# Linear attention with a two-of-eight expert network: rows of the second batch taken in pairs of one expert, with 256 moving columns

## The chip, the cores and the metric

The kernel runs on one core of a Trainium2 chip. The metric is the device time of one execution in microseconds (us), the median of several runs. The core has five engines that run at the same time, each on its own list of instructions: TensorE (PE, with the loads of its stationary operand shown apart as PEld), VectorE (DVE), ScalarE (ACT), GpSimd (POOL) and SyncE (SP), which issues DMA transfers. PE writes its results to PSUM; the kernel divides it into eight banks of 128 partitions by 512 float32 values, from which DVE and ACT read.

## What is computed

The input x has 8 sequences of 1024 tokens with 256 values each, so 8192 tokens, all in float32. The output is x plus an attention plus an expert network, both applied to the layer norm of x:

```python
xn = _layernorm(x, axis=-1)
# attention, 16 heads of 16 values
q = jax.nn.elu(xn @ Wq.T) + 1.0
k = jax.nn.elu(xn @ Wk.T) + 1.0
kv_cumsum = cumsum(k outer v, along the sequence)
out = q . kv_cumsum / clip(q . cumsum(k), 1e-06)
attn = out @ Wo.T
# experts: the two best of eight by logits, weights by a softmax over the two
y_e = (_silu(xn @ W1[e]) * (xn @ W3[e])) @ W2[e]      # 256 -> 512 -> 256
ffn = sum over the two experts of weight * y_e
return x + attn + ffn
```

The reference computes every expert for every token and weights most with zero. The kernel computes only the two chosen ones, so each token gives two rows of work, 16384 rows in all, which have to be sorted by expert.

## The kernel before

**Blocks and tiles.** Attention goes over 16 blocks of 512 tokens (NBLK, TB). The expert network goes over row tiles: 128 rows of one expert. Since each expert's last tile may be part empty, there are NF = 135 of them; the last NR = 3 are in a branch at the end that is taken only if they are needed, so that NM = 132 run. They come in two batches. The first has N1 = 25 tiles and holds rows of the first four blocks only, so that the expert network can start while the routing of the other blocks is still being computed. The second has N2 = 110 and is planned by `second_batch` (L696), a list of small DVE operations on counts of rows per expert (`left`, `upto`, `past`, `room`) and of matmuls (held_ps, L725) that give for each place of each tile its token.

**A row tile, step j of the main loop** (`ffn_step`, L1237). Step j issues: the gathers of tile j+3 (`ffn_load`, two indirect DMAs on POOL: the rows xg, L1145, and their norm and weight, entry, L1150); the two weight matrices of tile j+2 (`ffn_weights`, 512 KB each on SP's queue, five buffers w13); gate and up of tile j (`ffn_hidden`); the turning of tile j+1 (`ffn_turn`, two transposes xg_t on PE, L1166, and a copy xgT on ACT, L1168); the second matrix of tile j-1 (`ffn_out`, y_ps, L1218, then the scaling y on DVE, L1225); and the store of a finished tile (`ffn_store`, an indirect DMA on POOL that adds, L1229). Gate and up are 16 matmuls of 128 moving columns into two PSUM banks (gu_ps, L1199). In float32 each matmul is two PE instructions, so that is 32. ACT reads the gate's bank with Silu (L1207) and DVE multiplies it with the up bank into hT (L1210), which is what frees that bank.

**Attention** is a generator of 11 steps a block (`block_steps`, L993), 176 in all. `attend_upto` (L1021) advances it to a given step; the main loop calls it once a row tile, ahead of `ffn_step`. A block's first steps project q, k and v (zq L795, zkk and zkv L811, then Relu, Exp and products on ACT and DVE, L762 to L765) and its denominators: den (L880) is stored to DRAM as den_d and read back as rden through SP's queue. Then follow four chunks of 128 tokens. `scores` (L909) puts 16 PE instructions of scores into four banks at once (s_ps, L919); DVE masks each bank (s_sb, L926), which frees it; it also updates the state (kv_ps L934 on PE, kv L939 and L941 on DVE). `weigh` (L945) forms o_ps (L953, L960), and DVE multiplies it with rden into oT (L967). `attend` (L972) multiplies oT with the output matrix (a_ps, L979); ACT copies it (L984) and POOL adds a block to the output.

**PSUM.** ps_mm has four banks, shared in turn by gu_ps, s_ps, zq, zkk and zkv. ps_y has two, for y_ps and a_ps (and held_ps). ps_t has two, for xg_t, tp, kv_ps and o_ps. A matmul into a bank waits until the reader of the bank's content before has finished.

**The order.** Each engine works through its instructions in one fixed order. It comes from the order in the program and from a scheduler that may move instructions in the first part; what is marked by `in_order`, the DMAs on SP among it, stays as written. Normalising the blocks 4 to 15 (`turn`, L324, and its store of xnT to DRAM, L346) and their routing go on in the first 12 row steps; `second_batch` follows in ten steps from step 12 (LISTS, READ). From READ on, the steps of attention are spread evenly over the row tiles:

```python
attend_upto(AHEAD + (NBLK * STEPS - AHEAD) * (j - READ + 1) // (NM - READ - 4))
if j == N1 + 1:
    copied.append(j)
    in_order(nc.sync.dma_start(out=out_rows[0 : FT * P, :], in_=acc_d[:, :]))
ffn_step(j, LATE if N1 < j <= N1 + LATE else 0)
```

## Time and profile before

| | |
|---|---|
| device time, median of 3 runs | 1349.92 us (1348.86 to 1350.81) |
| the profiled execution: its own time, its span | 1333.92 us, 1332.0 us |
| granted TensorE clock | 0.992 |
| PE, PEld busy | 1279.3 us (96%), 1094.5 us (82%) |
| DVE, ACT, POOL busy | 635.0, 516.5, 528.2 us |
| DMA | 240.36 MB, mean 180 GB/s |
| loads of w1 and w3 | 264 of 512 KB |
| longest wait of PE, at the start | 11.0 us, tp L333 for DVE xb L313 |

All durations below come from one profiled execution, which has its own time; the span runs from its first to its last instruction. The busy time of an engine is a sum over instructions, and a share of it says nothing yet on what sets the end. Groups of instructions are written as line, engine, operation, output and inputs by the program's names, shapes, count, then busy time and mean duration. Matmuls overlap in the engine's pipeline, so the mean duration of one is longer than the distance from one to the next. In a list of waits, "A <- B: total, times, longest" says how long A's engine stood idle until B had finished. A chain of waits gives start, duration and what ran, followed back from an end; a timeline lists each group with, in brackets, the idle time before it and what ended it.

### The profile page before, as it was taken

To read this page: it belongs to the slowest core of one execution; us is meant where nothing else is said; L and a number is where in the kernel's file an instruction comes from. 1 tells how busy PE (TensorE), PEld (TensorE's weight loads), DVE (VectorE), ACT (ScalarE), POOL (GpSimd) and SP (SyncE) were. 2 spreads that over 40 slices of the span, in tenths; PEclk is the share of its full clock that TensorE was granted. 3 is DMA by queue.
4 is the path that set the end of the run, shared out by engine and by line. 5 is a ranking of instruction groups with operands and counts; after the bars stand their busy time and mean duration, and the time that the engine had idled before them with its cause. 6 is when DMAs were issued, how large, how long until landed. Compare 5 with 4: busy or idle time off the path is not lost.

```text
span 1332.0 us, 28306 instructions
## 1 busy us (share of the span) xinstructions
PE 1279.3 (96%) x10968; PEld 1094.5 (82%) x10968; DVE 635.0 (48%) x1436; ACT 516.5 (39%) x1052; POOL 528.2 (40%) x460
## 2 busy tenths in 40 slices
PE   5799999999999999999999999999999999999996
PEld 4578787878888788888888888888888888888885
DVE  7867498753353425353443535253533534252531
ACT  4666373531515142342516152432425151524321
POOL 3634433333334334344344434344344343343432
PEclk9999999999999999999999999999999999999998
DMA  9898756566776667576666766675766676576663
GB/s 339 276 297 238 201 162 180 127 179 174 205 201 169 173 142 204 134 195 166 151 188 144 201 164 178 160 195 146 176 165 150 176 175 183 144 198 148 179 163 76
DMA packets 163462, 240.36 MB, mean 180 GB/s; under 512 B 16098, under 2 KB 87394, under 8 KB 163042
## 3 DMA queue, kind: packets, MB, share of 16 engines
q1 hardware_dynamic: 119938, 184.31, 44.4%
q0 software_dynamic: 38064, 43.22, 20.1%
q10 hardware_dynamic: 5328, 11.01, 2.3%
q8 instruction: 90, 1.47, 0.4%
q14 instruction: 42, 0.34, 0.1%
HBM read 196.30 MB, written 52.67 MB: 187 GB/s over the span
## 4 chain that ended last, share of the span: by engine, by line
PE 86%; DVE 8%; DMA 3%; SPq 1%; issue 1%; ACT 1%; POOL 0%; POOLq 0%; DVEq 0%; ACTq 0%
PE gu_ps L1199 35%; PE y_ps L1218 16%; PE s_ps L919 6%; PE o_ps L960 4%; PE a_ps L979 4%; PE zq L795 4%; PE zkk L811 4%; PE zkv L811 3%; PE xg_t L1166 2%; PE kv_ps L934 2%; DVE s_sb L926 2%; PE o_ps L953 2%; DMA xb<-in_x_dram 2%; DVE ksum L863 1%; DMA acc_d<-in_x_dram 1%
## 5 line engine op out<-in xcount | busy, mean ns | idle before, releaser
L1199 PE MATMUL gu_ps<-xgT,w 128*128 128x128 f32 x4224 | 512.4, 278 | 4.6 <-DVE s_sb L926 2.8
L1199 PEld LDWEIGHTS gu_ps<-xgT,w 128*128 128x128 f32 x4224 | 492.3, 192 | 29.4 <-issue 15.7
L1145 POOL DMA_INDIRECT xg<-in_x_dram,src_i x132 | 131.9, 999 | 451.9 <-ACT xgT L1168 361.2
L1218 PE MATMUL y_ps<-w_sb,hT 128*128 x1056 | 251.8, 381 | 2.8 <-DVE hT L1210 2.5
L1229 POOL DMA_INDIRECT out_dram<-y,dst_i x107 | 173.8, 1624 | 164.8 <-DVE y L1225 71.5
L1210 DVE TENSOR_TENSOR hT<-gu_ps,hT 128x512 f32<-128x512 f32 x132 | 91.1, 690 | 272.0 <-PE gu_ps L1199 254.5
L1218 PEld LDWEIGHTS y_ps<-w_sb,hT 128*128 128x128 f32 x1056 | 190.7, 191 | 25.5 <-DVE hT L1210 2.7
L1207 ACT ACTIVATE hT<-gu_ps 128x512 f32<-128x512 f32 x132 | 78.8, 597 | 334.9 <-PE gu_ps L1199 332.7
L926 DVE TENSOR_TENSOR s_sb<-s_ps,causal 128x512 f32<-128x512 f32 x256 | 162.7, 682 | 52.6 <-PE s_ps L919 49.8
L1225 DVE TENSOR_SCALAR y<-y_ps,entry 128x256 f32<-128x256 f32 x132 | 63.6, 482 | 145.3 <-PE y_ps L1218 145.2
L1150 POOL DMA_INDIRECT entry<-tab_d,of_i x107 | 110.0, 1028 | 36.8 <-issue 31.7
L1168 ACT COPY xgT<-xg_t 128x256 f32<-128x256 f32 x132 | 49.1, 372 | 157.8 <-PE xg_t L1166 152.6
L919 PE MATMUL s_ps<-qm,kT 32*128 32x256 f32 x1024 | 95.4, 406 | 1.4 <-DVE hT L1210 0.4
L984 ACT COPY at<-a_ps 128x256 f32<-128x256 f32 x64 | 23.8, 371 | 170.7 <-PE a_ps L979 170.7
L919 PEld LDWEIGHTS s_ps<-qm,kT 32*128 32x128 f32 x1024 | 55.9, 183 | 31.2 <-issue 18.5
L1157 ACT ACTIVATE xg<-xg,entry 128x256 f32<-128x256 f32 x132 | 79.7, 603 | 3.6 <-DVE v L286 3.2
L1229 POOL DMA_INDIRECT acc_d<-y,src_i x25 | 43.5, 1742 | 76.9 <-DVE y L1225 47.4
L979 PE MATMUL a_ps<-wo_sb,oT 128*128 128x256 f32 x256 | 67.6, 386 | 5.6 <-DVE oT L967 5.4
L960 PE MATMUL o_ps<-s_sb,va 128*32 128x128 f32 x2048 | 72.3, 278 | 0.0
L960 PEld LDWEIGHTS o_ps<-s_sb,va 128*32 128x32 f32 x2048 | 53.2, 110 | 9.2 <-issue 0.9
L795 PE MATMUL zq<-xnT,wq_sb 128*128 128x512 f32 x128 | 60.2, 603 | 0.0
L979 PEld LDWEIGHTS a_ps<-wo_sb,oT 128*128 128x128 f32 x256 | 46.2, 190 | 16.8 <-DVE oT L967 9.7
(211 smaller groups left out, 1363.5 us busy)
## 6 DMA issues: line engine op xcount, KB each, us to landing
w<-in_w_dram SPq DMA_DIRECT2D x264, 512.0 KB
den_d<-over SPq DMA_DIRECT2D x64, 128.0 KB
rden<-den_d SPq DMA_DIRECT2D x16, 512.0 KB
xnT_d<-xnT ACTq DMA_DIRECT2D x15, 512.0 KB
xnT<-xnT_d SPq DMA_DIRECT2D x15, 512.0 KB
out_dram<-in_x_dram SPq DMA_DIRECT2D x12, 512.0 KB
out_dram<-at POOLq DMA_DIRECT2D x12, 512.0 KB, 8.2
xb<-in_x_dram SPq DMA_DIRECT2D x10, 512.0 KB
```

What stands on the lines that cost most here:

```text
L795: nc.tensor.matmul(z, lhsT=wq_sb[:, k, bass.ts(o, P)], rhs=xnTs[t][:, k, :], start=(k == 0), stop=(k == KC - 1),)
L811: nc.tensor.matmul(z[:, i, :], lhsT=xnTs[t][:, k, bass.ts(c + i, P)], rhs=wkv_sb[:, k, a, :], start=(k == 0), stop=(k == KC - 1),)
L919: nc.tensor.matmul(s_ps[r][:, hh].rearrange("p a l -> p (a l)"), lhsT=kT[rows, hh, span], rhs=qm[rows, hh, :, span], start=True, stop=True,)
L926: nc.vector.tensor_tensor(sm, s_ps[r].rearrange("p k a l -> p (k a) l"), causal_b, ALU.mult)
L960: nc.tensor.matmul(o_ps[32 * r : 32 * r + 32, hh, :], lhsT=va[:, c, 4 * hh + r, a, :], rhs=s_sb[r][:, 2 * hh + a, :], start=(first and a = ...
L979: nc.tensor.matmul(a_ps, lhsT=oT[:, hh, :], rhs=wo_sb[:, hh, :], start=(hh == 0), stop=(hh == 1),)
L1145: nc.gpsimd.indirect_dma_start(out=xg[j], out_offset=None, in_=x_rows[:, :], in_offset=bass.IndirectOffsetOnAxis(ap=src_i[:, i : i + 1], a ...
L1150: nc.gpsimd.indirect_dma_start(out=entry[j], out_offset=None, in_=table[:, :], in_offset=bass.IndirectOffsetOnAxis(ap=num_i[:, i : i + 1], ...
L1199: done = nc.tensor.matmul(ps[:, i, :], lhsT=w13[:, k, bass.ts(i, P)], rhs=xgT[j][:, k, :], start=(k == 0), stop=(k == KC - 1),)
L1210: nc.vector.tensor_tensor(hT, gu[1], hT, ALU.mult)
L1218: done = nc.tensor.matmul(y_ps, lhsT=hT[:, i, :], rhs=w2_sb[:, bass.ds(e * (IC * H) + i * H, H)], start=(i == 0), stop=(i == IC - 1),)
L1229: nc.gpsimd.indirect_dma_start(out=rows[:, :], out_offset=bass.IndirectOffsetOnAxis(ap=dst_i[:, i : i + 1], axis=0), in_=ys.pop(j), in_off ...
```

## The change

The second batch is cut in another way. ND = 48 pairs come first: two tiles of 128 rows of the same expert each. Then come 14 single tiles, the last three in the branch at the end, so 11 of them run. Where the loop went over 132 tiles, it goes over 84 units (`units`, NU): 25 singles of the first batch, 48 pairs, 11 singles.

- **A pair** has xgT and hT twice as wide, and its two weight matrices are loaded once. Gate and up have 256 moving columns. A bank then holds two of the four 128-row parts of the hidden layer, so `ffn_hidden` goes in two halves, each with one gate and one up bank, one Silu and one mult. `ffn_turn` makes four transposes and one copy; `ffn_out` makes two y_ps of eight instructions, as before.
- **Attention's steps**: the loop's single call becomes up to four for a pair, through `between`: ahead of the unit, between the halves, after the second half (ahead of `ffn_turn`), and between the two y_ps.
- **The planner** has more small operations: it counts pairs per expert, cuts them at ND, and forms starts and ends for pairs and singles apart.
- **Buffers**: entry has 12 instead of 8; the second-batch xnT has one instead of two. w13 and y keep five, xg four. Gathers run up to four tiles ahead, counted in tiles; LATE, by which stores are held back after the first batch, goes from 3 to 1.

```diff
+    ND = (2 * NT - N1 - E + 1) // 2
+    N2D = 2 * ND
...
-            xnT = (two if t == 0 else f_two).tile([P, KC, TB], F32, tag="xnT", name="xnT")
+            xnT = (two if t == 0 else f_one).tile([P, KC, TB], F32, tag="xnT", name="xnT")
...
         left = f_one.tile([P, E], F32, name="left")
         nc.vector.tensor_tensor(left, rows, taken, ALU.subtract)
-        upto = add_up(left, "upto2")
-        past = past_experts(upto, N2, f_x, "xb")
+        pairs_i = f_two.tile([P, E], I32, tag="rows_i", name="pairs_i")
+        nc.vector.tensor_copy(pairs_i, left)
+        nc.vector.tensor_scalar(pairs_i, pairs_i, 1, None, ALU.arith_shift_right)
+        pairs = f_one.tile([P, E], F32, name="pairs")
+        nc.vector.tensor_copy(pairs, pairs_i)
+        upto = add_up(pairs, "upto2")
+        nc.vector.tensor_scalar(upto, upto, float(ND), 2.0, ALU.min, ALU.mult)
+        ends = f_one.tile([P, E], F32, name="ends")
+        nc.vector.tensor_tensor(ends[:, 1:E], upto[:, 1:E], upto[:, 0 : E - 1], ALU.subtract)
+        nc.vector.tensor_copy(ends[:, 0:1], upto[:, 0:1])
+        nc.vector.tensor_tensor(ends, ends, taken, ALU.add)
+        nc.vector.tensor_tensor(left, rows, ends, ALU.subtract)
+        upto_s = add_up(left, "upto3")
+        nc.vector.tensor_scalar(upto_s, upto_s, float(N2D), None, ALU.add)
+        past = f_x.tile([P, N2, E - 1], F32, tag="xb", name="past")
+        nc.vector.tensor_copy(rows_left, upto_s[0:1, E - 1 : E])
+        parts = slice(0, N2D), slice(N2D, N2)
+        for part, ends_at in zip(parts, (upto, upto_s)):
+            n = part.stop - part.start
+            nc.vector.tensor_tensor(
+                past[:, part], cols[:, part].unsqueeze(2).to_broadcast([P, n, E - 1]),
+                ends_at[:, 0 : E - 1].unsqueeze(1).to_broadcast([P, n, E - 1]), ALU.is_ge,
+            )
         te, te_i = numbers_of(past, N2, "2")
-        nc.vector.tensor_copy(rows_left, upto[0:1, E - 1 : E])
...
+        for part, firsts_at, lasts in zip(parts, (taken, ends), (ends, rows)):
+            n = part.stop - part.start
+            room = f_two.tile([P, E - 1], F32, tag="room", name="room")
+            nc.vector.tensor_scalar(
+                room, lasts[:, 0 : E - 1], -1.0, float(ROWS), ALU.mult, ALU.add
+            )
+            nc.vector.tensor_tensor(room, room, firsts_at[:, 1:E], ALU.add)
+            nc.vector.tensor_tensor(
+                past[:, part], past[:, part], room.unsqueeze(1).to_broadcast([P, n, E - 1]),
+                ALU.mult,
+            )
+        of_tiles = f_one.tile([P, N2], F32, name="rows2")
+        nc.vector.tensor_reduce(of_tiles, past, op=ALU.add, axis=AX.X)
+        for part, first in zip(parts, (taken, ends)):
+            nc.vector.scalar_tensor_tensor(
+                of_tiles[:, part], of_tiles[:, part], first[:, 0:1],
+                cols[:, 0 : part.stop - part.start], ALU.add, ALU.add,
+            )
...
+    ffn4 = ctx.enter_context(tc.tile_pool(name="ffn4", bufs=4))
     ffn5 = ctx.enter_context(tc.tile_pool(name="ffn5", bufs=5))
-    ffn4 = ctx.enter_context(tc.tile_pool(name="ffn4", bufs=4))
-    ffn8 = ctx.enter_context(tc.tile_pool(name="ffn8", bufs=8))
+    ffn12 = ctx.enter_context(tc.tile_pool(name="ffn12", bufs=12))
...
+    units = [(j,) for j in range(N1)]
+    units += [(j, j + 1) for j in range(N1, N1 + N2D, 2)]
+    units += [(j,) for j in range(N1 + N2D, NF)]
+    NU = len(units) - NR
...
+    def ffn_turn(u):
+        n = P * len(units[u])
+        tp = ps_t.tile([P, KC, n], F32, tag="t", name="xg_t")
+        for r, j in enumerate(units[u]):
+            for k in range(KC):
+                nc.tensor.transpose(tp[:, k, bass.ts(r, P)], xg.get(j)[:, bass.ts(k, P)], ident)
+        xgT[u] = ffn2.tile([P, KC, 2 * P], F32, tag="xgT", name="xgT")[:, :, 0:n]
+        nc.scalar.copy(xgT[u], tp)
...
+    def ffn_hidden(u, between, last=False):
+        n = P * len(units[u])
+        m = TB // n
+        hT = ffn2.tile([P, IC, 2 * P], F32, tag="hT", name="hT")[:, :, 0:n]
+        for a in range(0, IC, m):
+            if a > 0:
+                between()
+            gu = []
+            for s in range(2):
+                if last and s == 1:
+                    ffn_out(u - 1, None, True)
+                ps = ps_mm.tile([P, m, n], F32, tag="mm", name="gu_ps")
+                for i in range(m):
+                    for k in range(KC):
+                        done = nc.tensor.matmul(
+                            ps[:, i, :], lhsT=ws[u, s][:, k, bass.ts(a + i, P)],
+                            rhs=xgT[u][:, k, :], start=(k == 0), stop=(k == KC - 1),
+                        )
+                        if last:
+                            in_order(done)
+                gu.append(ps)
+            half = hT[:, a : a + m, :]
+            silu = nc.scalar.activation(half, gu[0], AF.Silu)
+            if u == 0:
+                in_order(silu)
+            nc.vector.tensor_tensor(half, gu[1], half, ALU.mult)
+        del ws[u, 0], ws[u, 1]
+        hs[u] = hT
...
+    def ffn_out(u, between=None, last=False):
+        hT = hs.pop(u)
+        e = expert_of(units[u][0], mybir.EngineType.PE)
+        for r, j in enumerate(units[u]):
+            if r > 0:
+                between()
+            y_ps = ps_y.tile([P, H], F32, tag="y", name="y_ps")
...
+    def ffn_step(u, behind, between):
+        while loaded[0] < min(u + 4, NU) and units[loaded[0]][-1] - units[min(u, NU - 1)][-1] <= 4:
+            for j in units[loaded[0]]:
+                ffn_load(j)
+            loaded[0] += 1
+        if u + 2 < NU:
+            ffn_weights(u + 2)
+        if u < NU:
+            ffn_hidden(u, between, u == NU - 1)
+        if u < NU and len(units[u]) > 1:
+            between()
+        if u + 1 < NU:
+            ffn_turn(u + 1)
+        if u > 0 and u != NU - 1:
+            ffn_out(u - 1, between)
         for _ in range(2):
-            if stored[0] < j - behind:
+            if stored[0] < u - behind:
                 ffn_store(stored[0])
                 stored[0] += 1
...
-    LATE = 3
+    LATE = 1
...
         if j < LISTS:
-            attend_upto(3 + j // 2)
+            upto = [3 + j // 2]
         elif j < READ:
-            attend_upto(AHEAD - 2 * (READ - j - 1))
+            upto = [AHEAD - 2 * (READ - j - 1)]
         else:
-            attend_upto(AHEAD + (NBLK * STEPS - AHEAD) * (j - READ + 1) // (NM - READ - 4))
+            unit = units[min(j, NU - 1)]
+            n = 4 * len(unit) - 4 or 1
+            upto = [
+                AHEAD + (NBLK * STEPS - AHEAD) * (n * (unit[0] - READ + 1) + len(unit) * i)
+                // (n * (NM - READ - 4))
+                for i in range(n)
+            ]
+        goals = iter(upto)
+        attend_upto(next(goals))
         if j == N1 + 1:
             copied.append(j)
             in_order(nc.sync.dma_start(out=out_rows[0 : FT * P, :], in_=acc_d[:, :]))
-        ffn_step(j, LATE if N1 < j <= N1 + LATE else 0)
+        ffn_step(j, LATE if N1 < j <= N1 + LATE else 0, lambda: attend_upto(next(goals, 0)))
```

## The prediction

> **What bounds the kernel now.** I read first the page's busy times and costliest groups, then PE's waits, then the chain of work in one steady window, then three places where PE does lose time.
>
> From the page:
> ```profile
> PE 1279.3 (96%) x10968; PEld 1094.5 (82%) x10968; DVE 635.0 (48%) x1436; ACT 516.5 (39%) x1052; POOL 528.2 (40%) x460
> ...
> L1199 PE MATMUL gu_ps<-xgT,w 128*128 128x128 f32 x4224 | 512.4, 278 | 4.6 <-DVE s_sb L926 2.8
> L1199 PEld LDWEIGHTS gu_ps<-xgT,w 128*128 128x128 f32 x4224 | 492.3, 192 | 29.4 <-issue 15.7
> ...
> L1218 PE MATMUL y_ps<-w_sb,hT 128*128 x1056 | 251.8, 381 | 2.8 <-DVE hT L1210 2.5
> ...
> L919 PE MATMUL s_ps<-qm,kT 32*128 32x256 f32 x1024 | 95.4, 406 | 1.4 <-DVE hT L1210 0.4
> ```
> PE is busy 96% of the span; gate/up is its largest group and nearly all of its loads are covered (492.3/4224 = 117 ns each). PE's waits, by what ended them:
> ```profile
> PE a_ps L979 <- DVE oT L967: 5.4, 9, 0.9
> ...
> PE gu_ps L1199 <- DVE s_sb L926: 2.8, 3, 2.0
> PE y_ps L1218 <- DVE hT L1210: 2.5, 4, 0.9
> ```
> No wait for weights (w) is there, and past the first 50 us all waits are short. The chain of waits, 700 to 720 us (start, duration, what):
> ```profile
> 702.45 1.73 PE y_ps L1218 x8
> 704.18 0.86 PE a_ps L979 x4
> 705.04 3.43 PE zq L795 x8
> 708.47 3.57 PE gu_ps L1199 x32
> ```
> This is PE alone. From it the prices start to start: 128 moving columns 3.57/32 = 111.6 ns; 256 columns 1.73/8 = 216.1 ns; 512 columns 429 ns.
>
> PE loses time where the four score banks (s_ps) must first be read by DVE. The timeline at 320 us, a score set right behind gate/up:
> ```profile
> 320.46 0.71 PE L919 MATMUL s_ps<-qm,kT 32*128 32x256 f32 x6
> 320.64 0.69 DVE L1210 TENSOR_TENSOR hT<-gu_ps,hT 128x512 f32<-128x512 f32 x1 [5.31 <-PE gu_ps L1199]
> 321.38 1.13 PE L919 MATMUL s_ps<-qm,kT 32*128 32x256 f32 x10 [0.21 <-DVE hT L1210]
> 322.44 0.92 PE L1218 MATMUL y_ps<-w_sb,hT 128*128 x3
> ```
> The set takes 322.44 - 320.46 = 1.98 us, where a free set takes 1.11: 0.87 us lost until the mult on DVE has read the up bank. The chain at 365 us, two sets with only kv_ps between:
> ```profile
> 366.05 1.11 PE s_ps L919 x16
> 367.16 0.68 DVE s_sb L926
> 367.85 0.04 issue
> 367.89 2.92 PE s_ps L919 x16
> 370.81 0.64 PE kv_ps L934 x4
> ```
> The second set takes 2.92 instead of 1.11 (and kv_ps a little longer): 2.16 us lost. At 462 us it is the next step that is late:
> ```profile
> 462.97 0.60 DVE s_sb L926
> 463.57 0.34 DVE oT L967
> 463.91 0.04 issue
> 463.95 1.13 PE a_ps L979 x4
> ```
> a_ps waits because DVE does its masks before oT, about 0.78 us.
>
> **What the Trainium skill says.** "TensorE: Matmul & The Clock Gate", section Back-to-back issue gap: a warm matmul costs N/2.4 ns and 2.5 ns fixed. The trace has two column-times per instruction: 256/2.4 + 4.9 = 111.6 and 512/2.4 + 2.8 = 216.1. So wider matmuls save only a small fixed part; this agrees. Same page, section LDWEIGHTS: columns/1.2, 106.7 ns for 128; the trace's 117 lies just under 111.6 of streaming plus overlap, so at 128 columns loading and streaming are nearly equal, at 256 the load is half. "Trainium Kernel Development and Optimization", section Best Practices: consistent bubbles can mean that PSUM ran out; the 0.87 and 2.16 us places are that. "ScalarE: Activation LUTs", section What ACT_TABLE_LOAD costs: about 1283 ns; the trace has 1283 ns for 28 Silu loads.
>
> **The change part by part.** Counts of places come from the built instruction orders of both programs, past the first 290 us; the durations are from the profile.
>
> Gate/up of 96 row tiles become 48 pairs: removed 96 x 3.571 = 342.8 us, added 48 x 32 x 0.2161 = 331.9 us: **-10.9**.
>
> Weights: 96 of 264 loads of 512 KB go (50 MB of 240). PE waits for no load now: 0. PEld busy falls by 1536 x 117 ns = 180 us, hidden already: 0.
>
> Attention steps at half tiles move the score sets. (a) Four back-to-back pairs of sets disappear: 4 x 2.16 = **-8.6**. (b) The four places where a set comes between o_ps and a_ps go: 4 x 0.78 = **-3.1**; four waits of a_ps behind gate/up, 0.75, 0.38, 0.75 and 0.30, go too: **-2.2**. (c) gate/up followed by xg_t falls from 106 to 26 places; each carries a lag of 45 ns now: **-3.6**. (d) gate/up waiting for a mask behind kv_ps, 9 to 7 places of 0.36: **-0.7**. Together with the columns: -29.1.
>
> Against that: (e) sets directly behind a gate/up half rise from 0 to 20, at 0.87: **+17.4** (and 4 with a_ps between, 0.05 each: +0.2). A half still fills a gate and an up bank of 128x512, with Silu 0.60 and mult 0.69 us, so the price should carry over. Behind the waiting s_ps stands all of PE. Bounds: 0 if the two banks that it needs first were others, 1.5 if Silu is late as well (0.60 more). (f) xg_t behind o_ps now needs the ps_t bank of kv_ps, 10 places: DVE frees it some 2.4 us after the scores end, PE is there after 2.2 (8 places) or 1.56 (2): 8 x 0.2 + 2 x 0.86 = **+3.3**. (g) Two sets with xg_t and one y between: **+1.6**; y behind y in two banks: **+1.0**.
>
> The planner of the second batch has about 15 more small DVE operations of 0.15 to 0.16 us. DVE has no idle between 157 and 178 us, so they can show: 0 to 2.4, taken **+1.5**.
>
> Costed at nothing: Table loads on ACT, 58 to 66: 8 x 1.28 = 10.3 us on an engine that waits 332.7 us for PE ahead of Silu; uncovered, one makes a Silu 1.3 us late. The single buffer of xnT in the later normalisation: its store ends at most 6.1 us after issue and the next copy comes at least 6.1 us after; tightest spare 1.3 us, so 0 to +1. rden is queued on SP behind weights whose buffers come free only when a pair's second half is done: it takes 5.3 to 7.1 us, and in four blocks the slack shrinks to 2.6 to 4.7 us; oT is then up to 1.8 us late on DVE, with y's scaling and the next mult queued behind it. PE reads oT four us later, so 0; without that cover 4 x 1.8 = +7. POOL issues the same gathers, two at a time, and waits 361 us for ACT's copy today: 0. Fewer stores are held back (LATE 3 to 1): POOL only: 0.
>
> Sum: -29.1 + 25.0 = **-4.1 us**. The profiled execution took 1333.92 us with a span of 1332.0; the median 1349.92 lies 16.0 above it. I keep that difference: span 1327.9, profiled execution 1329.8, median **1345.8**.
>
> **Rivals.** Slower: the sets behind the halves cost more than they do today. With everything else as above, the sum turns at (29.1 - 7.6)/20 = 1.08 us per set. Place: the Silu of the half's gate on ACT, which may stand behind Exp, norms and a table load of 1.28 us; then Silu and mult are waited for in turn, 0.87 + 0.60 = 1.47, which adds 12.0: **1358**. For it: halves come at shorter distances and ACT gets 8 table loads more. Against: ACT is 39% busy and at 320 us it was the mult, not Silu, that ended last. The lost cover of rden would add up to 7 to this.
>
> Larger gain: the score banks come free earlier than I take it (half the price at the 20 places), and (f), (g) stay hidden as most short waits of this trace are: -8.7 - 5 more: **1332**. For it: the waits view puts all waits of s_ps at 0.8 us in the whole span. Against: the one place with the same order cost 0.87.
>
> No difference: the wide columns save 10.9 as worked out, but the moved steps cost as much as they free, with the waits merely changing place; **1350**, 1347.5 to 1352.5. For it: gains and losses of the moved steps (18.2 and 25.0) are nearly equal, and a 5% error in each cancels my net.
>
> **How the numbers follow.** Forecast as summed (1341 to 1350) 0.40; no difference 0.15; larger gain 0.12; slower 0.33. About 0.2%, 2.7 us, is what a measurement of this kernel can tell from no change. Faster: 0.12 + 0.33 of the forecast = 0.45; same: 0.07 + 0.13 = 0.20; slower 0.35. The range 1335 to 1361 takes in both ends of (e) but not all of rden's loss; the forecast's own is 1341 to 1350.
>
> **What would show it.** Gate/up of pairs at 216 ns start to start; sets behind a half of about 2.0 us, released by DVE's mult (right) or later ones by ACT's Silu (slower rival); no 2.9 us sets; xg_t waiting for DVE's kv; PEld busy near 915 us, 190 MB moved. I am wrong if PE starts to wait for w, for rden through oT, or for the gathers, or if the sets cost other than 0.6 to 1.1 us.

## The result: 1363.21 us, 1% slower

The changed kernel takes 1363.21 us (median of 6 runs, 1359.03 to 1371.58), the kernel before, run beside it, 1351.07 us: a ratio of 1.0099, with a 95% interval of 1.0074 to 1.0123. The prediction was 1345.8 us, faster; the time lies above its range of 1335 to 1361 us, and on the other side of the kernel before. The profiled execution of the changed kernel took 1363.07 us with a span of 1361.3.

One thing has to be known to read what follows: the kernel before takes about 1339 us in some groups of runs (a lower group) and about 1351 us in others (a higher group), and all kernels of a group shift with it, so each comparison below is with the runs of before in the same group. The profile that the prediction was made from was of the lower kind (1333.92 us), and so is the second group of experiments; the result and the other groups are of the higher. For reading the change against before I use the trace of the first experiment, called the stand-in below: the kernel before with one buffer less, which makes no difference, span 1349.7 us.

The page of the kernel after, its busy times and costliest groups:
```profile
PE 1284.0 (94%) x9432; PEld 1044.8 (77%) x9432; DVE 638.4 (47%) x1451; ACT 519.2 (38%) x1012; POOL 527.2 (39%) x460
...
PEclk9899999998999999999999999999999999999998
...
L1244 PE MATMUL gu_ps<-xgT,w 128*128 128x256 f32 (+1 forms) x2688 | 498.4, 340 | 5.8 <-DVE s_sb L957 5.0
L1244 PEld LDWEIGHTS gu_ps<-xgT,w 128*128 128x128 f32 x2688 | 429.5, 193 | 60.2 <-issue 14.0
```
Gate and up have 2688 instructions instead of 4224 and 14 us less of busy time than in the profile of before; 189.78 MB are moved instead of 240.36. But PE is busy 94% of a longer span. PE's waits, by what ended them:
```profile
PE a_ps L1010 <- DVE oT L998: 7.4, 10, 1.7
PE s_ps L950 <- issue: 6.3, 3, 5.8
...
PE s_ps L950 <- DVE hT L1255: 4.5, 19, 0.6
```
The third row is 19 of the 20 score sets behind gate/up halves, as forecast. The second holds one stall of 5.8 us and the first waits for oT of up to 1.7 us; the prediction had neither. The forecast price of a set can be read at 705 us (timeline: start, duration, instructions, then the idle time and its end):
```profile
705.42 0.71 PE L950 MATMUL s_ps<-qm,kT 32*128 32x256 f32 x6
705.59 0.69 DVE L1255 TENSOR_TENSOR hT<-gu_ps,hT 128x512 f32<-128x512 f32 x1 [3.62 <-PE gu_ps L1244]
706.34 1.13 PE L950 MATMUL s_ps<-qm,kT 32*128 32x256 f32 x10 [0.22 <-DVE hT L1255]
707.40 0.71 PE L965 MATMUL kv_ps<-va,kn 128*128 128x128 f32 x4
```
The set lasts 707.40 - 705.42 = 1.98 us, and DVE's mult releases it, exactly as at the one place of before.

**Where the time went.** I mark in each trace when row tiles 20 and 120, counted from 0, reach their y_ps. The stand-in: 302.8 and 1256.0 us. After: 317.8 and 1267.5. So 15.0 us are lost before tile 20, in a part of the program that does not yet work on a single pair, and the 100 tiles behind it, with the pairs, gain 3.5. The prediction had +1.5 for the first part (the planner) and -5.6 for the rest. It is the first part that it got wrong.

Three stretches of the first part carry the loss. Columns: stretch, its length, busy time and instructions of PE, PEld, DVE, ACT, POOL, then granted clock, DMA share and GB/s. First the kernel after, then the stand-in:
```profile
60.00:80.00 20.00, 12.32 (x86) 10.70 (x87) 9.98 (x61) 5.67 (x12) 8.26 (x8) 0.74 0.52 152
100.00:120.00 20.00, 17.82 (x132) 15.88 (x133) 14.04 (x58) 9.43 (x20) 6.13 (x6) 0.83 0.77 218
290.00:320.00 30.00, 23.60 (x160) 17.95 (x159) 15.09 (x34) 4.66 (x14) 11.35 (x11) 0.77 0.48 136
...
60.00:80.00 20.00, 16.08 (x136) 14.05 (x140) 10.36 (x56) 11.37 (x25) 4.42 (x5) 0.91 0.70 229
100.00:120.00 20.00, 20.00 (x207) 16.92 (x207) 14.07 (x54) 13.03 (x29) 7.11 (x6) 1.00 0.88 276
290.00:320.00 30.00, 27.78 (x239) 22.96 (x238) 10.56 (x19) 3.98 (x9) 7.95 (x7) 0.89 0.80 247
```
In each of them PE issues fewer instructions than the stand-in, at a lower clock. POOL is busier than there in the first and the last: 8.26 us against 4.42, and 11.35 against 7.95. This is the stretch at 300 us, in the timeline of the kernel after:
```profile
299.36 1.00 POOL L1181 DMA_INDIRECT entry<-tab_d,of_i  x1 [0.30 <-issue]
300.67 0.95 POOL L1181 DMA_INDIRECT entry<-tab_d,of_i  x1 [0.30 <-issue]
301.92 0.95 POOL L1181 DMA_INDIRECT entry<-tab_d,of_i  x1 [0.30 <-issue]
...
302.13 0.70 PE L950 MATMUL s_ps<-qm,kT 32*128 32x256 f32 x4
303.17 1.61 POOL L1280 DMA_INDIRECT acc_d<-y,src_i  x1 [0.30 <-issue]
305.09 0.98 POOL L1181 DMA_INDIRECT entry<-tab_d,of_i  x1 [0.30 <-issue]
306.38 0.95 POOL L1181 DMA_INDIRECT entry<-tab_d,of_i  x1 [0.30 <-issue]
308.01 0.60 ACT L1252 ACTIVATE hT<-gu_ps 128x512 f32<-128x512 f32 x1 [11.23 <-remote]
308.66 3.82 PE L950 MATMUL s_ps<-qm,kT 32*128 32x256 f32 x13 [5.83 <-issue]
```
The gate's matmuls end at 300.4 us by the trace, but Silu begins at 308.01, after ACT has done nothing for 11.23 us and 0.7 us after POOL's unbroken run of DMA issues has ended. PE stands for 5.83 us because Silu and the mult behind it still hold its banks. The entry gathers in this run reach tile 31, while gate and up are at tile 20: with 12 buffers of entry instead of 8 there is room for them at once, and the scheduler of the first part puts them ahead of the store.

At 62 to 68 us it is the same with another reader. PE's matmuls of the logits (lg_ps) wait for ACT's copies xnT of transposes that PE finished at 59.42 and 62.28 us; ACT makes them at 66.90 and 69.74, around the end of another unbroken run of POOL's (67.34 us):
```profile
66.90 0.59 ACT L341 COPY xnT<-tp 128x512 f32<-128x512 f32 x1 [4.83 <-remote]
...
67.54 0.65 PE L359 MATMUL lg_ps<-xnT,wr_sb 128*32 128x128 f32 x8 [4.60 <-issue]
```

### The profile page after: what moved, and what is told of

The parts are those of the page before. It is cut to its first block, busy times and chain, and to the rows that moved or that the text cites. A ratio compares the mean times of both kernels' runs of the same rounds, so it can differ in the third digit from the quotient of the medians.

```text
span 1361.3 us, 24495 instructions
## 1 busy us (share of the span) xinstructions
PE 1284.0 (94%) x9432; PEld 1044.8 (77%) x9432; DVE 638.4 (47%) x1451; ACT 519.2 (38%) x1012; POOL 527.2 (39%) x460
## 2 busy tenths in 40 slices
DMA packets 137333, 189.78 MB, mean 139 GB/s; under 512 B 14562, under 2 KB 85858, under 8 KB 136930
## 4 chain that ended last, share of the span: by engine, by line
PE 81%; DVE 9%; ACT 5%; issue 2%; DMA 1%; another core or an unknown queue 1%; POOL 0%; POOLq 0%; DVEq 0%; ACTq 0%
PE gu_ps L1244 32%; PE y_ps L1267 15%; PE s_ps L950 5%; PE o_ps L991 5%; PE a_ps L1010 4%; PE zq L826 4%; PE zkv L842 3%; PE zkk L842 3%; PE xg_t L1206 2%; PE kv_ps L965 2%; PE o_ps L984 2%; DVE hT L1255 1%; DVE s_sb L957 1%; ACT L794 1%; DVE ksum L894 1%
## 5 line engine op out<-in xcount | busy, mean ns | idle before, releaser
L1244 PE MATMUL gu_ps<-xgT,w 128*128 128x256 f32 (+1 forms) x2688 | 498.4, 340 | 5.8 <-DVE s_sb L957 5.0
L1244 PEld LDWEIGHTS gu_ps<-xgT,w 128*128 128x128 f32 x2688 | 429.5, 193 | 60.2 <-issue 14.0
L950 PE MATMUL s_ps<-qm,kT 32*128 32x256 f32 x1024 | 102.3, 417 | 10.9 <-issue 6.3
L1208 ACT COPY xgT<-xg_t 128x512 f32<-128x512 f32 (+1 forms) x84 | 41.5, 494 | 165.2 <-PE xg_t L1206 156.9
L950 PEld LDWEIGHTS s_ps<-qm,kT 32*128 32x128 f32 x1024 | 58.9, 187 | 46.2 <-issue 27.3
L1195 ACT ACTIVATE xg<-xg,entry 128x256 f32<-128x256 f32 x132 | 74.2, 598 | 4.0 <-DVE sq L303 3.0
L991 PEld LDWEIGHTS o_ps<-s_sb,va 128*32 128x32 f32 x2048 | 54.1, 110 | 11.3 <-issue 2.9
```

The costliest lines, as they stand in the source:

```text
L950: nc.tensor.matmul(s_ps[r][:, hh].rearrange("p a l -> p (a l)"), lhsT=kT[rows, hh, span], rhs=qm[rows, hh, :, span], start=True, stop=True,)
L991: nc.tensor.matmul(o_ps[32 * r : 32 * r + 32, hh, :], lhsT=va[:, c, 4 * hh + r, a, :], rhs=s_sb[r][:, 2 * hh + a, :], start=(first and a = ...
L1244: done = nc.tensor.matmul(ps[:, i, :], lhsT=ws[u, s][:, k, bass.ts(a + i, P)], rhs=xgT[u][:, k, :], start=(k == 0), stop=(k == KC - 1),)
```

## The experiments

What could have cost the time: the score sets behind the halves at more than their price; a buffer made single (xnT) or held longer (w13); rden late behind the weights; and for the first part the planner's operations, the place in memory of the weights, and POOL's list with its deeper buffers of entry. Each was timed beside the kernel before; "ratio" is to before in its group. The first group holds one buffer of xnT, the steps behind the turn, the two sizes together and rden on POOL; the second the weights, the eight buffers, the planner and all three together; the third the repetitions and the eight buffers again; the fourth the rest. The second group is the lower one. The expectations speak of theories as they stood when they were written; where they speak of chips, read groups, since the second and the third ran on the same chip and were of different kinds.

**One buffer of xnT, alone** (the kernel before with this one line):
```diff
-            xnT = (two if t == 0 else f_two).tile([P, KC, TB], F32, tag="xnT", name="xnT")
+            xnT = (two if t == 0 else f_one).tile([P, KC, TB], F32, tag="xnT", name="xnT")
```


> The kernel before with the buffer of xnT of blocks 4 to 15 alone changed from two to one. Theory (the single buffer makes ACT wait for the store, PE idles around 60 us and its clock falls): the tenth y_ps group is reached 10 to 16 us later than in the kernel before, the median is 8 to 16 us longer. Rival (the stalls at 58 to 70 us of the changed kernel have another cause, the store is hidden): within 3 us of the kernel before.

Measured: 1350.18 us, ratio 0.9999 (0.9988 to 1.0011). The rival holds: the single buffer costs nothing, as the prediction had it.

**Attention's steps behind the turn.** The changed kernel, with the call between the halves removed, so that no score set stands directly behind a half:
```diff
             if a > 0:
-                between()
...
-        if u < NU and len(units[u]) > 1:
-            between()
         if u + 1 < NU:
             ffn_turn(u + 1)
+        if u < NU and len(units[u]) > 1:
+            between()
...
-            n = 4 * len(unit) - 4 or 1
+            n = 3 * len(unit) - 3 or 1
```


> The changed kernel with three places for attention steps in a pair, none of them right behind a gate/up half: ahead of the unit, behind the transposes, between the two y_ps. Theory (20 score sets behind a half cost 0.9 us each): 10 to 18 us faster than the changed kernel, hardly any s_ps set of 2.0 us left. Rival (the sets lose their time wherever they stand, since DVE is what they wait for): within 4 us of the changed kernel, with the waits at other places.

Measured: 1341.07 us, ratio 0.9933 (0.9908 to 0.9958). Repeated beside the changed kernel itself:

> The changed kernel once more, beside the kernel before on the chip that this call gets; the kernel before takes 1351 us on one chip here and 1339 us on another. Theory (the change costs the first 300 us and the waits for oT only where PE's semaphore updates come late, which shows as fewer recorded updates of PE's semaphore than PE raises, 1266 of 1355 in the first trace): if the updates are complete in this trace, 3 to 8 us faster than the kernel before, as e5 and e6 were; if some 90 are missing, 10 to 15 us slower. Rival (the placement of the weights and the entry gathers made e5 and e6 faster): 10 to 15 us slower than before on either chip.

> The changed kernel with the attention steps behind the transposes and between the two y_ps (as in the second experiment), on the chip of this call. Theory (the 20 score sets behind gate/up halves cost 0.9 us each on any chip): 10 to 22 us faster than the changed kernel of this call. Rival (that gain belonged to the chip of the first call): under 8 us.

Measured: the changed kernel 1362.58, ratio 1.0082 (1.0055 to 1.0108), 11.3 us slower, as was expected for a trace without some 90 updates (it has 1267 of 1355; what these are comes below); the steps behind the turn 1342.93, ratio 0.9926 (0.9898 to 0.9954). Removing the 20 sets and what goes with them (one place for steps less, another moved) is worth 19.7 us, within what was expected, against 17.4 that the prediction charged for the sets. The gain comes where it should; in the first of the two runs tile 20 is at 316.3 us (317.8 in the changed kernel), tile 120 at 1245.9 (1267.5). There the wait for the mult shrinks to what is left elsewhere (waits of PE):
```profile
PE s_ps L950 <- DVE hT L1253: 3.1, 3, 1.9
```
So the price was about right, and it was a price that need not be paid. But tile 20 is as late as ever: the first part's loss has another cause.

**Two buffers of xnT and four of weights, in the changed kernel:**
```diff
-            xnT = (two if t == 0 else f_one).tile([P, KC, TB], F32, tag="xnT", name="xnT")
+            xnT = (two if t == 0 else f_two).tile([P, KC, TB], F32, tag="xnT", name="xnT")
...
-            ws[u, s] = ffn5.tile([P, KC, I], F32, tag="w13", name="w13")
+            ws[u, s] = ffn4.tile([P, KC, I], F32, tag="w13", name="w13")
```


> The changed kernel with two buffers of xnT, paid for with four instead of five buffers of weights (w13). Theory (the single xnT buffer is what costs the first 160 us): the eightieth y_ps instruction is back near 158 us from 173.6, the median 8 to 16 us below the changed kernel. Rival (the weights wait with four buffers, or the stalls are not of xnT): no gain, or PE waits for w. In both, the steady part from 340 us on stays as it is.

Measured: 1359.21 us, ratio 1.0059 (1.0035 to 1.0083), whose interval overlaps that of the changed kernel; the 8 to 16 us that were expected are not there. The two changes together do not undo the loss. Four buffers of weights were not tried alone.

**rden read through POOL's queue** instead of SP's, where it stands behind weights:
```diff
-            nc.sync.dma_start(
+            nc.gpsimd.dma_start(
```


> The changed kernel with the read of rden issued on POOL's queue instead of SP's, past no weights. Theory (oT waits for an rden that is queued behind weights): the 6.4 us that y_ps loses ahead of a_ps, and waits of a_ps for oT of up to 1.7 us, go: 5 to 7 us faster. Rival (oT is late because DVE has the masks and mults of the half tiles ahead of it): these waits stay, within 2 us.

Measured: 1404.74 us, ratio 1.0404 (1.0386 to 1.0421), some 41 us slower than the changed kernel where 5 to 7 us of gain were expected, with this among PE's waits:
```profile
PE a_ps L1010 <- DVE oT L998: 40.1, 18, 5.0
```
On POOL the read stands behind gathers, and comes later: DVE stands 32.4 us for rden ahead of oT, 0.7 in the kernel after. So on SP's queue, behind the weights, it is hardly late.

**Weights placed early.** In the changed kernel the first load of weights starts late, because the memory that the weights get was used by something else before. SP's list around the first w, kernel after:
```profile
36.58 0.62 SPq L1151 DMA_DIRECT2D tab_d<-tab  x1
41.43 3.27 SPq L1222 DMA_DIRECT2D w<-in_w_dram  x4
```
In before it starts at 34.82 us in the profile that the prediction used (the first trace below), and at 36.14 in the stand-in. The experiment opens the pools in another order, so that w13 gets memory that is free early:
```diff
+    ffn5 = ctx.enter_context(tc.tile_pool(name="ffn5", bufs=5))
     ffn4 = ctx.enter_context(tc.tile_pool(name="ffn4", bufs=4))
-    ffn5 = ctx.enter_context(tc.tile_pool(name="ffn5", bufs=5))
+    ffnh = ctx.enter_context(tc.tile_pool(name="ffnh", bufs=2))
...
-        hT = ffn2.tile([P, IC, 2 * P], F32, tag="hT", name="hT")[:, :, 0:n]
+        hT = ffnh.tile([P, IC, 2 * P], F32, tag="hT", name="hT")[:, :, 0:n]
```


> The changed kernel with the same instructions but another order of the buffer pools in SBUF: xgT first, then the weights and y, then xg, then hT in a pool of its own. The weights then lie where the kernel before has them, and not behind the wider xgT and hT, where an early tile is read until 41 us. Theory (the first expert weights are late because of where their buffers lie: first load at 41.4 us instead of 36.1): they start near 36 us again, the tenth and twentieth tiles are 4 to 8 us earlier than in the changed kernel, the median is 4 to 10 us below it. Rival (the first loads are covered; the loss lies in the planner and at 300 us): within 2 us of the changed kernel.

Measured: 1333.11 us, ratio 0.9957 (0.994 to 0.9973), with the first load where it was before:
```profile
36.16 0.39 SPq L1223 DMA_DIRECT2D w<-in_w_dram  x1
```
Of the 4 to 10 us that were expected against the changed kernel nothing can be said: it was not run in this group. In the same group, **eight buffers of entry** in the changed kernel:
```diff
-    ffn12 = ctx.enter_context(tc.tile_pool(name="ffn12", bufs=12))
+    ffn12 = ctx.enter_context(tc.tile_pool(name="ffn12", bufs=8))
```


> The changed kernel with eight instead of twelve buffers of entry; the built order differs on POOL alone. Theory (the gathers of entry that run ahead in a bunch near 300 us, five of them in front of a store, belong to the stall of 5.8 us that PE has there and to the half-speed clock behind it): the stall shrinks to under 2 us, 4 to 9 us faster than the changed kernel. Rival (POOL only happens to be busy then): the stall and the time stay within 2 us.

Measured: 1331.18 us, ratio 0.9945 (0.9925 to 0.9965), again without the changed kernel beside it; against that, only POOL's order is another. Its waits of PE:
```profile
PE s_ps L950 <- DVE hT L1255: 5.1, 22, 0.6
...
PE a_ps L1010 <- DVE oT L998: 0.3, 1, 0.3
```
The waits for oT, 7.4 us in the kernel after, are gone, although rden is read at the same place behind the weights. The weights placed early, with twelve buffers of entry, show the same (0.7 us). So rden's place was not enough to make oT late, which was the cover that the prediction worried about. The trace of the kernel after shows what it was late for:
```profile
575.46 1.08 PE L991 MATMUL o_ps<-s_sb,va 128*32 128x128 f32 x32
576.42 1.61 POOL L1280 DMA_INDIRECT out_dram<-y,dst_i  x1 [0.30 <-issue]
578.34 0.99 POOL L1181 DMA_INDIRECT entry<-tab_d,of_i  x1 [0.30 <-issue]
579.73 0.42 DVE L998 TENSOR_TENSOR oT<-rden,o_ps 128x256 f32<-128x256 f32 x1 [4.12 <-PE y_ps L1267]
580.21 1.13 PE L1010 MATMUL a_ps<-wo_sb,oT 128*128 128x256 f32 x4 [1.74 <-DVE oT L998]
```
PE has finished o_ps at 576.54; DVE begins 3.2 us later, when POOL's two issues are over. It looks the same as at 300 us: what PE has finished is acted on by the other engines only after POOL's issuing. The traces record semaphore updates (the signals by which one engine tells the others that an instruction is done), and tell the two kinds of groups apart. Of the updates that PE's instructions should raise, there are 1338 of 1339 in the first trace of before, and all of them, to within three, in the group just shown; 1195 of 1339 in the stand-in, and 1266 of 1355 in the kernel after. Of the stand-in's 144 missing ones 138 fall inside POOL's issues of indirect DMAs, to 0.06 us; in the kernel after about 70 of some 90. Of those that are recorded, 61 in the stand-in lie over 0.25 us behind the end of their instruction, in the first trace none. It is not PE alone: DVE's updates are 1247 of 1371 in the stand-in and ACT's 854 of 887, where the first trace has them all.

The weights placed early hold a control that settles what the run of gathers does by itself. That kernel has the twelve buffers, and POOL the same nine issues in the same order near 290 us, but its updates are complete:
```profile
288.94 1.03 POOL L1182 DMA_INDIRECT entry<-tab_d,of_i  x1 [0.30 <-issue]
290.06 0.60 ACT L1253 ACTIVATE hT<-gu_ps 128x512 f32<-128x512 f32 x1 [3.70 <-PE gu_ps L1245]
290.28 0.94 POOL L1182 DMA_INDIRECT entry<-tab_d,of_i  x1 [0.31 <-PE gu_ps L1245]
...
292.66 1.13 PE L950 MATMUL s_ps<-qm,kT 32*128 32x256 f32 x10 [0.21 <-DVE hT L1256]
292.78 1.61 POOL L1281 DMA_INDIRECT acc_d<-y,src_i  x1 [0.30 <-DVE hT L1256]
```
Silu starts in the middle of the run, 0.04 us behind the gate's matmuls (290.02), and PE waits 0.21 us instead of 5.83. At 60 to 80 us PE is busy for 18.89 of 20 us there, at full clock, though POOL's run lasts until 67.75 us. So neither stall comes with the twelve buffers alone; the updates have to be late as well. Nor is it the early weights that prevent them: the kernel before has its weights as early (35.74 us), and given twelve buffers in a higher group it stalls (below).

**Work for the planner, alone.** 19 operations like those that the change adds, about 3 us of DVE, put into `second_batch` of the kernel before without any effect on its numbers:
```diff
+        pairs_i = f_two.tile([P, E], I32, tag="rows_i", name="pairs_i")
+        nc.vector.tensor_copy(pairs_i, left)
...
+        for _ in range(5):
+            nc.vector.tensor_scalar(ends, pairs, 48.0, 2.0, ALU.min, ALU.mult)
+            nc.vector.tensor_tensor(pairs, ends, taken, ALU.add)
+            nc.vector.tensor_tensor(ends, pairs, pairs, ALU.subtract)
+        nc.vector.tensor_tensor(left, left, ends, ALU.add)
```


> The kernel before with 19 more small DVE operations in the planner of the second batch, at the place where the changed kernel has its own, and without any effect on the numbers. Theory (DVE is full there and PE waits for it): 3 to 6 us slower than the kernel before, the twentieth tile 3 to 6 us later. Rival (the operations find room behind PE's other work): within 1.5 us.

Measured: 1347.11 us, ratio 1.0058 (1.0041 to 1.0074): 8.3 us for 3 us of work, more than the 3 to 6 that were expected. In the first 330 us the trace has 34.1 us at half clock, the first trace of before 13.7. The order of the first part shifts with the added work, so this is not the price of the operations alone; it shows how far a small delay there can be magnified.

**All three together**: steps behind the turn, weights placed early, eight buffers of entry.

> The changed kernel with all three: attention steps behind the transposes and between the two y_ps instead of behind gate/up halves, the weights' buffers placed as in the kernel before, eight buffers of entry. Theory (the three losses are separate): 1341 us of the step placement alone less 4 to 10 us for the weights and 4 to 9 us for the stall near 300 us, so 1322 to 1333 us. Rival (the first 300 us lose their time to the planner and to the clock whatever the buffers): 1338 to 1342 us.

Measured: 1323.04 us, ratio 0.9882 (0.9866 to 0.9899). It lies in the expected range by luck, since that was counted from 1341 us of a higher group. And in a higher group, where the changed kernel had been slower than before:

> The changed kernel with steps behind the transposes and between the two y_ps, the weights placed as in the kernel before and eight buffers of entry, on the machine as this call finds it. Theory (the three parts add up in either state): 1.0 to 2.0% faster than the kernel before, so 1324 to 1338 us where the kernel before takes 1351, and 1318 to 1326 where it takes 1339. Rival (the gains overlap where updates come late): 0.7% or less, about the 1342 us of the step placement alone.

Measured: 1336.15 us, ratio 0.989 (0.9871 to 0.991), as the theory had it. This version beats the kernel before in either kind of group, by 1.1 to 1.2%.

**The buffers of entry alone, both ways.** First eight buffers in the changed kernel, in the group of its repetition above:

> The changed kernel with eight buffers of entry, on the chip of this call, beside the changed kernel itself. Theory (the bunch of gathers on POOL matters only where PE's updates are late): with complete updates within 3 us of the changed kernel; with updates missing, 4 to 9 us faster, and the stall at 300 us smaller. Rival (it is the entry buffers on any chip): 15 us or more faster than the changed kernel.

Measured: 1350.64 us, ratio 0.9996 (0.9985 to 1.0008), 11.9 us less than the changed kernel beside it: more than the theory's 4 to 9 us, less than the rival's 15. Then twelve in the kernel before:
```diff
-    ffn8 = ctx.enter_context(tc.tile_pool(name="ffn8", bufs=8))
+    ffn8 = ctx.enter_context(tc.tile_pool(name="ffn8", bufs=12))
```


> The kernel before with twelve instead of eight buffers of entry; the built order differs on POOL alone. Theory (the buffers alone make the bunch of gathers, and with PE's updates late PE stalls near 300 us): where updates are missing from the trace, 6 to 13 us slower than the kernel before and a PE wait of 4 to 6 us near 295 us; where they are complete, within 3 us. Rival (it takes the pairs as well): within 2 us of the kernel before everywhere.

Measured: 1364.47 us, ratio 1.0098 (1.0081 to 1.0115), 13.9 us slower, just over the 6 to 13 that were expected. This one number of buffers, with no pairs, no wide columns and no moved steps, costs as much as the whole change did. Tile 20 is reached at 316.2 us (317.8 in the kernel after), and near 305 us PE waits 3.54 us for Silu and 2.42 for the mult. With eight buffers in the changed kernel the three stretches look nearly as they did before:
```profile
60.00:80.00 20.00, 16.66 (x139) 14.25 (x139) 11.30 (x69) 8.62 (x19) 5.49 (x6) 0.83 0.72 207
100.00:120.00 20.00, 19.92 (x205) 16.77 (x206) 13.99 (x54) 13.48 (x29) 7.12 (x6) 1.00 0.82 248
290.00:320.00 30.00, 27.65 (x230) 22.91 (x229) 10.94 (x20) 3.91 (x8) 8.04 (x8) 0.89 0.77 233
```
and at 295 us (timeline) the store comes three entries earlier, one gather follows it, Silu is 5 us less late, and PE waits 0.91 us instead of 5.83:
```profile
291.56 1.61 POOL L1280 DMA_INDIRECT acc_d<-y,src_i  x1 [0.30 <-issue]
293.48 0.98 POOL L1181 DMA_INDIRECT entry<-tab_d,of_i  x1 [0.30 <-issue]
...
295.31 0.60 ACT L1252 ACTIVATE hT<-gu_ps 128x512 f32<-128x512 f32 x1 [6.33 <-PE gu_ps L1244]
...
295.96 1.85 PE L950 MATMUL s_ps<-qm,kT 32*128 32x256 f32 x12 [0.91 <-ACT hT L1252]
```

**Each entry gather twice**, in the kernel before from tile N1 + 3 on, some 104 more issues on POOL:
```diff
-        nc.gpsimd.indirect_dma_start(
+        for _ in range(2 if j >= N1 + 3 else 1):
+            nc.gpsimd.indirect_dma_start(
```


> The kernel before with each gather of entry of the second batch from its fourth tile on issued twice into the same tile, about 104 more of 1.0 us on POOL, which is 40% busy. Theory (while POOL issues a gather, PE's updates come late, and what waits for them starts late): where updates are missing, 4 to 12 us slower, with longer waits of PE for DVE; where complete, within 2 us. Rival (POOL's gathers only coincide with the late updates): within 2 us in both.

Measured: 1368.89 to 1392.07 us in four runs; the two shortest, 1368.89 and 1382.61, give the ratio 1.0183 (1.0121 to 1.0245), which is more than the 4 to 12 us that were expected. The trace is of the longest. In it PE's waits for oT are this, 9.4 us in the stand-in:
```profile
PE a_ps L979 <- DVE oT L967: 13.9, 10, 3.3
```
More issues on POOL, which is busy 39% of the span, make the kernel slower in a higher group. That agrees with the cause; but the spread forbids a price per issue, and a lower group, where the theory has no loss, was not tried.

## Why the prediction was wrong

**The step that failed** is "POOL issues the same gathers, two at a time, and waits 361 us for ACT's copy today: 0". The gathers are the same, but with 12 buffers of entry, which the sum does not have at all, some of them are issued earlier, in one run. The prediction compared the orders past 290 us only, and looked at POOL's idle time, not at what stands in its list ahead of a store, nor at who needs a signal while POOL issues. Measured in higher groups: 11.9 us in the changed kernel (1362.58 - 1350.64), 13.9 us in the kernel before (1364.47 - 1350.61). At 62 to 68 us ACT's copies xnT come later, at 300 us Silu.

A part of it is TensorE's clock. The Trainium skill, "TensorE: Matmul & The Clock Gate", section What's actually happening, says that PE is at half rate after an idle window of about 3.4 us. The traces agree in part. The time at half clock comes in multiples of 3.41 us, and in the kernel after it began at 306.2 us, behind 3.41 us in which PE stood still for 3.38. But no such window is needed: with eight buffers it began at 299.3 us, behind 3.41 us with 0.51 of standing still, and of 103 stretches at half clock in the sixteen traces (without the programs' ends) 18 follow 3.41 us in which PE stood still for less than 1. Here the measurement decides: a stall far shorter than the page's can stand ahead of the half clock.

What the 13.5 us before tile 20 consist of (317.8 against 304.3 with eight buffers) can be counted from the records of PE and of the clock, from 14 us on. PE stands still for 35.9 us instead of 26.7, so 9.2 more, of which the stall at 300 us is 4.9 (5.83 - 0.91). And 28.5 us of its work instead of 18.2 are done at half clock, which costs half of the difference, 5.2. In the repetition of the changed kernel the two parts are 7.6 and 7.2, of 14.2 us. So the clock is four to five tenths of the loss.

**The rest of the sum, where it can be seen alone**, is the changed kernel with eight buffers of entry against before. In the higher group tile 20 is at 304.3 against 302.8 us, +1.5, where the forecast had +1.5; from there to tile 120 it is -3.5, forecast -5.6. In the lower group the same marks give +4.5 (297.3 against 292.8 in the first trace) and -8.6, so that the first agreement is luck. Its time against before: -0.6 us in one group and -7.4 in the other (0.9945). The forecast of -4.1 lies between them, in neither interval. So the arithmetic had about the right size for what it covered, and no more can be said. Point by point:

- Gate/up, -10.9: the price held. 16 instructions take 3.47 us at 702 us, 216.9 ns each. Weights: 168 loads, and no wait for w among PE's waits: held.
- Sets behind the halves, +17.4 (0.87 each): held. 19 of the 20 take 1.98 us and one 2.33, together 17.7 us more than free sets of 1.11. DVE's mult releases them, so the slower rival, in which Silu is late, did not come true in the steady part. Without them, and with the steps placed otherwise, the kernel gains 19.7 us. The four sets of 2.9 us are gone, as forecast.
- xg_t behind o_ps, +3.3: too high. Past 330 us PE waits 0.6 us in all for kv ahead of xg_t.
- The a_ps waits that were to go (-3.1 and -2.2): they go where the updates come on time, from 5.4 us in all to 0.3 with eight buffers. In the higher groups the place of the wait merely changes, 9.4 to 7.4 us. rden behind the weights, costed at 0, was right in the lower group; in the higher ones oT was late behind POOL's issues.
- xnT's single buffer, 0: held. The planner, +1.5: DVE's work there went from 13.5 to 16.1 us, +2.6; what it costs in time was not separated.
- Not foreseen: the first load of weights 5 us later, from the order of the pools. The early placing brings it back to 36.16 us; what that is worth alone is open, since the changed kernel was not run in that group.
- "PEld busy near 915" was wrong, 1044.8: a load's record lasts longer beside wider matmuls (160 ns of busy time each instead of 117). It costs nothing, but a busy time per load was not a price.
- "The median lies 16.0 above" the profiled execution: this was no overhead, but the profile and the median were of two kinds of runs. The profiled execution of the kernel after lies 0.14 us below its median. The sum should have been made against a profile of the same kind as the median.
- Three slips of the working, none of them the step that failed. 117 ns of loading lies above 111.6 ns of streaming, not just under it. In the rival "no difference", moved steps that cost as much as they free would leave the -10.9 of the columns, and 18.2 and 25.0 are not nearly equal. And an error of 5% in each of these is 2.2 us together, half of the net of 4.1.

**What stays open.** That the number of buffers costs the time in a higher group is shown both ways; that late updates carry it rests on where the missing updates lie, on readers that start about when POOL ends, and on the run of nine issues that delays nothing where the updates are complete. What inside the chip makes them late, and why a group of runs has it or not, no run here shows. Whether the changed kernel as it stands is slower than before in a lower group was not run. LATE was not tried alone.

## What to carry to other kernels

A deeper pool need not be free: it lets what fills it run ahead in the list of the engine that issues it, and here what stood behind it there, or was signalled meanwhile, came later. Price it by looking at the built order from the start of the program, on the list that fills it, not only in the steady part where the change is meant to work. And put the steps that need a bank where the bank's reader is done already: behind the turn instead of between the halves, moving the same steps was worth 1.4% of this kernel.

## What the runs showed of the hardware

- While POOL issues indirect DMAs (0.95 to 1.0 us for a gather, 1.6 us for an accumulating store), readers on ACT and DVE of what PE has finished may start only about when the issuing ends: 7.6 us late at 300 us (308.01 - 300.4), 3.2 us late at 576 us. In the lower group the same run of nine issues delays Silu by 0.04 us, and the kernels are faster there by 12.5 us (the kernel before), 13.1 (all three together) and 19.5 (the changed kernel with eight buffers).
- With the delay go missing updates, of all three engines: in the stand-in 144 of PE's 1339, 124 of DVE's 1371 and 33 of ACT's 887; in the lower group at most 6 of any.
- The stall of 5.8 us came with 13.7 us at half clock between 290 and 330 us, where the kernel with eight buffers, which stalls 0.9 us there, has 6.8.
